# Third and fourth value product by a two-level scheme, and where its rooms and weight sums go

## The chip, the core and the metric

One Trainium2 chip, and one of its cores. The metric is the device time of one execution in microseconds, given as the median of three runs, with one profiled execution beside them.

## The reference

One RWKV block and a gated MLP over 2048 tokens of width 512, all in float32:

```python
x = x + rwkv(layernorm(x))          # time mix, then channel mix
x = x + ffn(layernorm(x))
# time mix: h = LN(x); k, v, r from h mixed with the token before; x += (sigmoid(r) * a/b) @ Wo.T
# channel mix:
h  = LN(x); hh = shift(h)
kk = (h * cm_mk + hh * (1 - cm_mk)) @ Wkey.T        # 512 -> 2048
kv = silu(kk) @ Wval.T                              # 2048 -> 512, the value product
sr = sigmoid((h * cm_mr + hh * (1 - cm_mr)) @ Wcr.T)
x  = x + sr * kv
# ffn: gate, up = h @ w_gate_up.T (512 -> 2 x 2048); out = (silu(gate) * up) @ w_down.T
```

The MLP's weights are other ones than the channel mix's, but the shapes of the value product and of the MLP's down product are the same: 512 tokens by 2048 by 512 in each block.

## The kernel before

The 2048 tokens are four blocks of 512. The kernel first runs time mix and channel mix for all blocks, then the MLP for all blocks. Between the two, each block's result goes to device memory (`resid`) and is loaded again.

**One-level products.** Nearly every product is a `unit` (L539): a Strassen-Winograd scheme of seven products on halves instead of eight. The operands are halves B11, B12, B21, B22 and the differences T1 to T4 (`sums_of`, L464), four VectorE subtractions on 128x512. The weights are halves A11, A12, A22, A21 and the sums S1 to S4. A half product is four matmuls of 128x128 by 256 columns for each of the unit's groups (L558). The value product is a unit with four groups (`down_unit`, L1031), so 7 x 4 x 4 matmuls. Its sink multiplies by the gate and adds to the residual with two `scalar_tensor_tensor` a result.

**Two-level products.** The MLP's down product (`down_product`, L1163) applies the scheme twice. It runs seven half products in the order of `DOWN` (n = 0 to 6), each of them as seven quarter products of four matmuls by 128 columns (L1212). The seven steps of an n are called `first` to `seventh`. They need quarter sums of the operand (`quarter_sums`, L1152: T1, T2, T4 and T3, four subtractions each, written to the tiles `quads` and `quad`, for T3 from n = 2 on in place into `hid`). The sums for n + 2 are asked for in the seventh step of n. A third step reads T2. ScalarE copies each quarter result out of PSUM (L1224), VectorE combines them (`rest`, L1248, and `seventh`), and `summed` (L1166) adds the half results: p1, p3, u2, u4.

Steps six and seven of an n are held back: they are issued between the first and third step of the next n, so that PE runs first(n), sixth(n-1), second(n), seventh(n-1), third(n), fourth(n), fifth(n). The last three products of a `unit` are held back in the same way.

**Weight sums.** The sums S are made on the chip once per weight. `prepare` (L146) loads four pieces on the POOL queue, makes four subtractions on VectorE and stores four pieces to device memory, again on the POOL queue. For a two-level product, each of its weights A11, A12, A22, S1 to S4 gets quarter sums of its own ("dd"), for which the S of the whole weight ("d") come first. Five ticks pass between the loads and the first subtraction. Preparations run in the order of `early` and `late`, at a pace given by `credit` per tick. `need_sums` forces one that is asked for and not ready.

**Who decides the order.** PE, VectorE and ScalarE execute in the order in which the code issues instructions. A planner in the code (`tick`, L295) keeps a slack: each PE step grants 0.88 of its length (1.72 us, half of that in `down_product`) and each VectorE instruction takes its cost off. Background work (norms, mixes) and urgent work (`hot`, the sums) is issued while the slack is above zero. Where a product needs a sum that is not yet issued, `run_one(True)` issues it on the spot, whatever stands before it. Weights arrive on SP's queue into a ring of twelve tiles of 256 KB (`wring`).

**Rooms.** SBUF is given out in pools. `q` (30 tiles of 128x512) and `htp` serve the mixes and are closed after the first gate unit of the MLP (`mixes.close()`, then `last_room`), where the pools of the MLP open: `hidden` (7 large tiles), `quads`, `fq`. Three operand rooms (`opp`) hold mixes, z operands and later the quads; `op_free` lets a mix start only when fewer than three are in use.

## Time and profile before

| | |
|---|---|
| median of three runs | 1238.54 us (1237.72 to 1238.57) |
| profiled execution, first to last instruction | 1237.6 us |
| granted TensorE clock, mean | 0.998 |
| TensorE busy | 1228.9 us, 99% |
| VectorE busy | 711.9 us, 58% |
| ScalarE busy | 358.0 us, 29% |
| moved by DMA | 293.27 MB, 237 GB/s |

The time of the profiled execution is its span, 1237.6 us, from the first to the last instruction; the three runs have their own times, which lie 0.1 to 1.0 us above it. PE is the matmuls, PEld the weight loads that run beside them. A float32 matmul stands as two records in the profile. A group is named by line, engine, operation and tiles, out<-in.

### The profile page before, as it was taken

How to read it: one execution, taken by the hardware profiler on the slowest of the kernel's cores; microseconds unless marked ns; L12 is line 12 of the kernel's file. 1: busy time of each engine (PE TensorE's matmuls, PEld its weight loads, DVE VectorE, ACT ScalarE, POOL GpSimd, SP SyncE). 2: the span in 40 equal slices, each digit the busy share in tenths (PEclk: the TensorE clock that was granted, in tenths of full speed). 3: DMA queues.
4: the chain of work that ended last, by engine and by line, in shares of the span. 5: the costliest groups of instructions: out<-in, count | busy, mean ns of one | idle time of the engine just before them, and what ended most of it. 6: DMA issues, size and time to landing. Idle time of an engine off the chain costs nothing.

```text
span 1237.6 us, 18092 instructions
## 1 busy us (share of the span) xinstructions
PE 1228.9 (99%) x6524; PEld 1101.8 (89%) x6524; DVE 711.9 (58%) x1315; ACT 358.0 (29%) x663; POOL 153.1 (12%) x278
## 2 busy tenths in 40 slices
PE   8999999999999999999999999999999999999998
PEld 7888888888888888888888888998899888998898
DVE  5877686587684757533542365556546365563466
ACT  5534352252532425202311222212221222112211
POOL 1332221222212121222100000000000000000000
PEclk9999999999999999999999999999999999999999
DMA  5768995889877887898756645895459755785576
GB/s 184 255 216 281 311 314 199 307 310 316 276 245 246 291 273 241 261 319 301 248 143 191 215 144 157 270 334 154 143 182 310 271 145 149 239 300 156 153 217 209
DMA packets 139871, 293.27 MB, mean 237 GB/s; under 512 B 17528, under 2 KB 18696, under 8 KB 138504
## 3 DMA queue, kind: packets, MB, share of 16 engines
q1 hardware_dynamic: 116736, 219.20, 56.2%
q0 software_dynamic: 21440, 70.27, 15.5%
q10 hardware_dynamic: 1608, 2.65, 0.6%
q8 instruction: 53, 0.87, 0.3%
q14 instruction: 34, 0.28, 0.1%
HBM read 250.11 MB, written 41.95 MB: 236 GB/s over the span
## 4 chain that ended last, share of the span: by engine, by line
PE 96%; DVE 2%; ACT 1%; DMA 1%; issue 0%; DVEq 0%
PE ps L558 54%; PE ps L1212 14%; PE accv L558 11%; PE accx L558 11%; PE ps L660 5%; PE ps L443 1%; DVE e L395 0%; DMA w<-in_w 0%; DVE mix L395 0%; DMA x<-in_x 0%; ACT mix L873 0%; ACT hT_a L865 0%; DVE q L387 0%; ACT mix L496 0%; DVE st L401 0%; DVE resid L387 0%
## 5 line engine op out<-in xcount | busy, mean ns | idle before, releaser
L558 PE MATMUL ps<-zT,w 128*128 128x256 f32 x1280 | 289.5, 379 | 0.0
L558 PEld LDWEIGHTS ps<-zT,w 128*128 128x128 f32 x1280 | 241.9, 190 | 32.2
L558 PE MATMUL ps<-mix,w 128*128 128x256 f32 x920 | 210.7, 379 | 0.0
L558 PEld LDWEIGHTS ps<-mix,w 128*128 128x128 f32 x920 | 174.5, 190 | 23.6
L387 DVE TENSOR_TENSOR u<-u,accx 128x512 f32<-128x512 f32 x66 | 45.2, 686 | 115.5 <-ACT accx L593 115.5
L1212 PE MATMUL ps<-w,hid 128*128 128x128 f32 x832 | 104.5, 275 | 0.0
L558 PE MATMUL ps<-w,t 128*128 128x256 f32 x456 | 102.2, 379 | 0.0
L1212 PEld LDWEIGHTS ps<-w,hid 128*128 128x128 f32 x832 | 99.8, 192 | 0.8
L558 PEld LDWEIGHTS ps<-w,t 128*128 128x128 f32 x456 | 86.4, 190 | 11.7
L1212 PE MATMUL ps<-w,quads 128*128 128x128 f32 x704 | 89.0, 275 | 0.4 <-ACT r L1224 0.4
L578 ACT COPY accv<-ps 128x512 f32<-128x512 f32 x66 | 37.7, 570 | 176.5 <-PE ps L558 175.4
L1212 PEld LDWEIGHTS ps<-w,quads 128*128 128x128 f32 x704 | 84.2, 192 | 0.9 <-ACT r L1224 0.5
L593 ACT COPY accx<-ps 128x512 f32<-128x512 f32 x66 | 37.7, 571 | 153.7 <-PE ps L558 152.0
L387 DVE TENSOR_TENSOR u<-ps,u 128x512 f32<-128x512 f32 x66 | 45.6, 691 | 62.6 <-PE ps L558 62.2
L387 DVE TENSOR_TENSOR raw<-raw 128x512 f32<-128x512 f32 x92 | 63.3, 688 | 20.1 <-DMA raw<-d 10.7
L589 ACT COPY u<-ps 128x512 f32<-128x512 f32 x66 | 38.6, 585 | 122.9 <-PE ps L558 122.9
L660 PE MATMUL ps<-mix,w 128*128 128x256 f32 x320 | 72.4, 386 | 1.1 <-DVE mix L395 1.1
L1224 ACT COPY r<-ps 128x128 f32<-128x128 f32 x112 | 29.8, 266 | 142.1 <-PE ps L1212 142.1
L660 PEld LDWEIGHTS ps<-mix,w 128*128 128x128 f32 x320 | 61.4, 194 | 10.2 <-DVE mix L395 1.8
L1306 POOL DMA_DIRECT2D out<-resid x12 | 8.6, 716 | 491.5 <-DVE resid L387 491.5
L558 PE MATMUL accv<-zT,w 128*128 128x256 f32 x256 | 60.6, 379 | 0.0
L558 PE MATMUL accx<-zT,w 128*128 128x256 f32 x256 | 60.5, 379 | 0.0
(168 smaller groups left out, 1654.4 us busy)
## 6 DMA issues: line engine op xcount, KB each, us to landing
w<-sum SPq DMA_DIRECT2D x312, 256.0 KB, 3.4
w<-in_w SPq DMA_DIRECT2D x254, 256.0 KB, 3.8
w<-dd SPq DMA_DIRECT2D x112, 256.0 KB, 3.6
raw<-in_w POOLq DMA_DIRECT2D x48, 256.0 KB, 5.5
sum<-raw POOLq DMA_DIRECT2D x48, 256.0 KB, 4.2
w<-d SPq DMA_DIRECT2D x48, 256.0 KB, 3.7
q<-in_w POOLq DMA_DIRECT2D x36, 256.0 KB, 6.3
sum<-q POOLq DMA_DIRECT2D x36, 256.0 KB, 4.7
```

Of the source, the lines that this page charges most:

```text
L387: nc.vector.tensor_tensor(out, a, b, op)
L443: nc.tensor.transpose(flat[:, t * P : (t + 1) * P], h[:, t, c * P : (c + 1) * P], ident)
L558: mm = nc.tensor.matmul(pz[:, m, :], lhsT=lhsT, rhs=rhs, start=first and g == 0 and m == 0 and k == 0, stop=g == last and k == 1, skip_gro ...
L578: "z", A11, B11, True, pop_held, read=lambda: nc.scalar.copy(accv, acc["z"])
L589: nc.scalar.copy(tmp["u2"], acc["z"])
L593: nc.scalar.copy(accx, acc["z"])
L660: mm = nc.tensor.matmul(acc[i, j][:, m, :], lhsT=act[:, k, lo] if by_token else wg[:, k, lo], rhs=wg[:, k, :] if by_token else act[:, k, : ...
L1212: mm = nc.tensor.matmul(dst, lhsT=x[k][:, g, :], rhs=wt[:, g, :], start=first and g == 0, stop=g == 3, skip_group_check=True,)
L1224: nc.scalar.copy(st["r"][:, m, n * P : (n + 1) * P], st["z"])
L1306: eng.dma_start(out_t[b][:, tokens, cols], rs[b][:, tokens, cols])
```

## The change

The value product of blocks 2 and 3 (`b >= DEEP`) goes through `down_product`, with quarter weights of its own: `wv` (quarters of the four halves, laid out on the host), `vsum` (the S sums of the four value weights, stored so that quarters can be read from them as pieces of 128 columns) and "vv" (the quarter sums). The seven "vv" preparations stand ahead of the MLP's in `late`. The MLP's preparations are no longer all forced before the MLP starts but go on in it. `credit` is 1.0 from block 2's gate unit to the end of its up units and the same in block 3, 0 during the two products, and 1.0 in the MLP. In block 2, after the gate unit and the next block's out unit, the mix pools close and the rooms for `hidden` and `quads` open, with waits by tile; one operand room goes to the quads from there on. Gates, and from block 3 on e and t tiles, come from the pool `up`, which grows from 6 to 10 tiles; `q` shrinks from 30 to 25. The first MLP operand (`ffn_in(0)`) is pushed after the first up unit of block 3 instead of after the last.

```diff
-    up = ctx.enter_context(tc.tile_pool(name="up", bufs=6))
+    up = ctx.enter_context(tc.tile_pool(name="up", bufs=10))
+    prep = ctx.enter_context(tc.tile_pool(name="prep", bufs=6))
...
+    vsum = [
+        dram.tile([P, 4, 2, HB], F32, tag=f"vsum{s}", name=f"vsum{s}") for s in range(4)
+    ]
+    for g in range(4):
+        sums[WVAL + g] = [flat(t[:, g]) for t in vsum]
+
+    def value_part(q, k):
+        if q < 4:
+            return wv[q, k].rearrange("p (g c) -> p g c", c=P)
+        m, kk = divmod((0, 1, 3, 2)[k], 2)
+        return vsum[q - 4][:, :, kk, m * P : (m + 1) * P]
+
+    for q in (A11, A12, A22, S1, S2, S3, S4):
+        sources["vv", q] = [value_part(q, k) for k in range(4)]
+        sums["vv", q] = scratch(f"vv{q}", 4)
...
+    def value_weight(q, k):
+        if k >= 4:
+            need_sums(("vv", q))
+            return ring(sums["vv", q][k - 4]).rearrange("p a (h c) -> p (a h) c", c=P)
...
+        nc.sync.dma_start(t, value_part(q, k))
+        return t
...
+    def value_up(b, g):
+        hid = hidden.setdefault((b, "v"), {})
+        def sink(i, j, c):
+            q = (B11, B12, B21, B22)[2 * i + j]
+            if q not in hid:
+                hid[q] = hidden_tile()
+            nc.scalar.activation(hid[q][:, g], c, AF.Silu)
+            if g == 3:
+                made.add(((b, "v"), q))
+                if q in (B11, B22):
+                    quarter_sums((b, "v"), 0 if q == B11 else 1)
...
     def up_unit(b, g):
+        if b >= DEEP:
+            value_up(b, g)
+            return
...
+        if b >= DEEP:
+            down_product((b, "v"), sink, value_weight, False, done)
+            return
         unit([WVAL + g for g in range(4)], [Lazy((b, g)) for g in range(4)], sink, True, done)
...
+    def deep_room():
+        def pool(stack, name, bufs):
+            return stack.enter_context(
+                tc.tile_pool(name=name, bufs=bufs, reuse_waits="tile")
+            )
+        room["hidden"] = pool(ctx, "hidden", 7)
+        more = pool(ctx, "more", 1)
+        ctx.enter_context(middle)
+        pools["ht"] = pool(middle, "htl", 1)
+        m, _ = op_tile("quads")
...
-    late = [n + g for g in range(4) for n in (WG, WU)] + [("dd", A11)]
+    late = [("vv", q) for q in (A11, S4, S2, A12, S1, S3, A22)]
+    late += [n + g for g in range(4) for n in (WG, WU)] + [("dd", A11)]
...
+        if b >= DEEP:
+            credit[1] = 1.0
         gate_unit(b)
         if b + 1 < NB:
             out_unit(b + 1)
+        if b == DEEP:
+            need((b, "ck"))
+            mixes.close()
+            deep_room()
...
+            if b == NB - 1 and g == 0:
+                push((0, "z", "t"), ffn_in(0), op_free)
...
-        if b == NB - 1:
-            push((0, "z", "t"), ffn_in(0), op_free)
+        if b >= DEEP:
+            credit[1] = 0.0
         down_unit(b)
...
-    while preps:
-        need_sums(preps[-1][0])
+    credit[1] = 1.0
     need((0, "z"))
     ffn_gate(0, 0)
-    mixes.close()
     last_room()
```

In the changed kernel the matmul lines L558 and L1212 are L600 and L1312, the VectorE add and subtract L387 is L429, `scalar_tensor_tensor` L395 is L437, and the copy out of PSUM L1224 is L1324.

More of the change, by code (lines that the diff above doesn't have):

```diff
@@ L35 @@
 TURNED = 2
+DEEP = 2
 PLAIN = {(0, WK), (0, WR), (0, WV), (0, WO), (1, WK), (1, WR)}
@@ L69, in rwkv_ffn_kernel @@
     wd: bass.AP,
+    wv: bass.AP,
     out: bass.AP,
@@ L90, in rwkv_ffn_kernel, with ht_tile @@
     mixes = ctx.enter_context(ExitStack())
-    htp = mixes.enter_context(tc.tile_pool(name="htp", bufs=2))
-    prep = mixes.enter_context(tc.tile_pool(name="prep", bufs=6))
-    pools = {"q": mixes.enter_context(tc.tile_pool(name="qp", bufs=30))}
+    pools = {
+        "ht": mixes.enter_context(tc.tile_pool(name="htp", bufs=2)),
+        "q": mixes.enter_context(tc.tile_pool(name="qp", bufs=25)),
+    }
+    def ht_tile(name):
+        return pools["ht"].tile([P, NC, TB + 1], F32, tag="hT", name=name)
     def q_tile(name):
@@ L150, in prepare @@
             t = prep.tile([P, 2, HB], F32, tag="raw", name="raw") if own else q_tile("q")
-            paced(nc.gpsimd.dma_start(flat(t), sources[n][k]))
+            src = sources[n][k]
+            dst = flat(t)
+            if len(src.shape) == 3:
+                dst = dst.rearrange("p (g c) -> p g c", c=P)
+            paced(nc.gpsimd.dma_start(dst, src))
             raw.append(t)
@@ L186, in down_weight @@
         return ring(src).rearrange("p a (h c) -> p (a h) c", c=P)
+    def value_weight(q, k):
+        if k >= 4:
+            need_sums(("vv", q))
+            return ring(sums["vv", q][k - 4]).rearrange("p a (h c) -> p (a h) c", c=P)
+        if q >= 4:
+            for g in range(4):
+                need_sums(WVAL + g)
+        t = wring.tile([P, 2, HB], F32, tag="w", name="w")
+        t = t.rearrange("p a (h c) -> p (a h) c", c=P)
+        nc.sync.dma_start(t, value_part(q, k))
+        return t
     def load_x(b, queues=None):
@@ L768, in time_norm @@
         yield from scaled(xb, h, mv, both)
-        hT = htp.tile([P, NC, TB + 1], F32, tag="hT", name="hT_a")
+        hT = ht_tile("hT_a")
         hTs[b, "a"] = hT
@@ L804, in turned_norm @@
         tails[b] = residual(b, xb, [(mv[:, t, 0:1], rstd[:, t : t + 1]) for t in range(NT)])
-        hT = htp.tile([P, NC, TB + 1], F32, tag="hT", name="hT_a")
+        hT = ht_tile("hT_a")
         hTs[b, "a"] = hT
@@ L825, in first_block @@
         xb = xin.pop(0)
-        hT = htp.tile([P, NC, TB + 1], F32, tag="hT", name="hT_a")
+        hT = ht_tile("hT_a")
         hTs[0, "a"] = hT
@@ L928, in sink @@
                 ts(r[:, o, :], c[:, o, :], nfirst[:, n : n + 1], 0.0, ALU.subtract, ALU.min)
-            e = q_tile("e")
+            e = (u_tile if b > DEEP else q_tile)("e")
             q[i, j] = e
@@ L953, in hidden_sums @@
             for t in (T1, T2, T4):
-                B[t] = q_tile("t")
+                B[t] = (u_tile if key[0] > DEEP else q_tile)("t")
             B["sums"] = set()
@@ L983, in rwkv_ffn_kernel @@
     gates = {}
+    wide = []
     def channel_norm(b):
@@ L994, in channel_norm @@
         yield from scaled(x1, h, mv, rstd)
-        hT = htp.tile([P, NC, TB + 1], F32, tag="hT", name="hT_b")
+        hT = ht_tile("hT_b")
         hTs[b, "b"] = hT
@@ L1004, in sink @@
         def sink(i, j, c):
-            s = q_tile("sr")
+            if b == DEEP:
+                if not wide:
+                    wide.append(tok_tile("sr"))
+                s = wide[0][:, 2 * i + j, :].rearrange("p (m c) -> p m c", m=2)
+            else:
+                s = u_tile("sr")
             nc.scalar.activation(s, c, AF.Tanh, scale=0.5)
@@ L1009, in gate_unit @@
         product_of(b, WCR, "cr", sink, True)
+    def value_up(b, g):
[9 more added lines that the diff above has]
+                    quarter_sums((b, "v"), 0 if q == B11 else 1)
+        unit(
+            [WKEY + g],
+            [Lazy((b, "ck"))],
+            sink,
+            False,
+            lambda: hidden_done((b, "v"), g),
+            op_done if g == 3 else None,
+        )
     def up_unit(b, g):
+        if b >= DEEP:
+            value_up(b, g)
+            return
         s = {}
@@ L1085, in ffn_gate @@
         s = gated[b, g] = {}
-        tile_of = u_tile if (b, g) == (0, 0) else q_tile
+        tile_of = q_tile if g % 2 else u_tile
         def sink(i, j, c):
@@ L1108, in sink, with hidden_done @@
                     quarter_sums(b, 0 if q == B11 else 1)
-        def done():
-            if g == 0:
-                for t in (T1, T2, T4):
-                    hid[t] = hidden_tile()
-            urgent((b, "f", g), sums_of({t: hid[t][:, g] for t in hid}))
-            if g == 3:
-                made.update((b, t) for t in (T1, T2, T4, "T3"))
-        unit([WU + g], [Lazy((b, "z"))], sink, False, done, op_done if g == 3 else None)
+        unit(
+            [WU + g],
+            [Lazy((b, "z"))],
+            sink,
+            False,
+            lambda: hidden_done(b, g),
+            op_done if g == 3 else None,
+        )
+    def hidden_done(b, g):
+        hid = hidden[b]
+        if g == 0:
+            for t in (T1, T2, T4):
+                hid[t] = hidden_tile()
+        urgent((b, "f", g), sums_of({t: hid[t][:, g] for t in hid}))
+        if g == 3:
+            made.update((b, t) for t in (T1, T2, T4, "T3"))
     hidden, made, asked = {}, set(), set()
@@ L1128, in hidden_tile @@
         return room["hidden"].tile([P, 4, 2, HB], F32, tag="hid", name="hid")
-    def last_room():
-        room["hidden"] = ctx.enter_context(tc.tile_pool(name="hidden", bufs=7))
-        pools["q"] = ctx.enter_context(tc.tile_pool(name="fq", bufs=15))
-        more = ctx.enter_context(tc.tile_pool(name="more", bufs=1))
+    middle = ExitStack()
+    def deep_room():
+        def pool(stack, name, bufs):
+            return stack.enter_context(
+                tc.tile_pool(name=name, bufs=bufs, reuse_waits="tile")
+            )
+        room["hidden"] = pool(ctx, "hidden", 7)
+        more = pool(ctx, "more", 1)
+        ctx.enter_context(middle)
+        pools["ht"] = pool(middle, "htl", 1)
         m, _ = op_tile("quads")
@@ L1139, in last_room @@
         room["sets"] = tiles[:4], tiles[4:]
+    def last_room():
+        middle.close()
+        pools["q"] = ctx.enter_context(
+            tc.tile_pool(name="fq", bufs=4, reuse_waits="tile")
+        )
     def quarters(t):
@@ L1161, in quarter_sums, with down_product @@
         urgent((b, "quarters", n), run())
-    def down_product(b, sink, final):
+    def down_product(b, sink, weight_of, final, done=None):
         base = {}
@@ L1195, in summed @@
                 sink(1, 0, base["u2"])
+                if done is not None:
+                    done()
         def steps(n):
@@ L1209, in product @@
                         run_one(True)
-                wt = down_weight(a, q)
+                wt = weight_of(a, q)
                 for g in range(4):
@@ L1318, in sink @@
                 store(0, slice(HB, HB + P))
-        down_product(b, sink, final)
+        down_product(b, sink, down_weight, final)
     early = [WV, WCR, WO] + [WKEY + g for g in range(4)] + [WVAL, WVAL + 1]
-    late = [n + g for g in range(4) for n in (WG, WU)] + [("dd", A11)]
+    late = [("vv", q) for q in (A11, S4, S2, A12, S1, S3, A22)]
+    late += [n + g for g in range(4) for n in (WG, WU)] + [("dd", A11)]
     late += [("d", k) for k in range(4)] + [("dd", q) for q in (S4, S2, A12, S1, S3, A22)]
@@ L1363, in rwkv_ffn_kernel @@
             out_unit(b + 1)
+        if b == DEEP:
+            need((b, "ck"))
+            mixes.close()
+            deep_room()
         need((b, "ck"))
@@ L1457, in _layout @@
     )
+    down = val
+    wv = np.stack(
+        [np.stack([quarter_quarter(i, j, m, k) for m, k in places]) for i, j in places]
+    )
     return {
@@ L1463, in _layout @@
         "wd": np.ascontiguousarray(wd),
+        "wv": np.ascontiguousarray(wv),
     }
```

## The prediction

> **What bounds it now.** I read the busy times first, then the chain that ended last, then stretches, then the order in time of one two-level product. Page, part 1:

> ```profile
> PE 1228.9 (99%) x6524; PEld 1101.8 (89%) x6524; DVE 711.9 (58%) x1315; ACT 358.0 (29%) x663; POOL 153.1 (12%) x278
> ```

> PE is busy all through; DVE has room on average. So time falls only where PE gets less to do, and rises where PE is made to wait. The chain of work that ended last, in order of time, gives PE's pace for the two matmul widths:

> ```profile
> 594.60 6.91 PE ps L558 x32
> ...
> 778.62 39.30 PE ps L1212 x352
> ...
> 920.92 39.30 PE ps L1212 x352
> ```

> L558 is the 256-column matmul of a one-level unit: 6.91 / 32 = 215.9 ns a record (two records to a matmul). L1212 is the 128-column one of the two-level product: 39.30 / 352 = 111.6 ns, back to back for 39 us. Half the width costs 0.517 of the time.

> The stretches of the third value product (first line) and of the first MLP down product (second), columns as PE, PEld, DVE, ACT, POOL, clock, DMA share, GB/s:

> ```profile
> 503.00:552.00 49.00, 49.00 (x229) 43.14 (x228) 19.56 (x30) 5.30 (x9) 10.23 (x19) 1.00 0.88 300
> 778.62:817.92 39.30, 39.30 (x354) 39.30 (x353) 25.55 (x48) 7.02 (x25) 1.98 (x3) 1.00 0.90 297
> ```

> Neither stretch has a PE gap. The two-level form keeps DVE 65% busy and DMA at 0.90; both were affordable there.

> **What PE saves.** A value product is 7 products x 4 groups x 4 matmuls = 112 of 256 columns, 224 records: 224 x 215.9 ns = 48.4 us. At two levels it is 49 x 4 = 196 of 128 columns, 392 records: 392 x 111.6 = 43.8 us. That is 4.6 us saved in each, 9.2 us in blocks 2 and 3. The order of the built kernel confirms the counts (224 fewer 256-column matmuls, 392 more 128-column ones) and changes no other PE work.

> **What DVE gets.** Per product: 28 quarter sums of 0.69, seven each of 0.29, 0.29 and 0.425 for combining, seven adds of 0.69: 31 us, less the unit's two u2 operations (1.4 us). Once: seven preparations of four subtractions, 28 x 0.69 = 19.3 us, with 56 more POOL DMA issues of 0.54 us. In all 2 x 29.8 + 19.3 = 79 us, to about 64% of the span. The preparations go ahead of the MLP's, in block 1 and the start of block 2, where DVE was about 70% busy; the MLP's move back by as much, and the last eight end during the MLP of block 0 (32 subtractions, 22 us, in 99 us that hold 51 us of DVE work: 76.65 in the stretch 778 to 921 less 25.55). No weight is asked for before its preparation ended in the built order, so neither PE nor SP waits for one: 0. If that cover failed, a wait like the longest now on a preparation's load (9.8 us, DVE for raw<-d) would stand before the gated products; PE rode through it then, and with DVE fuller perhaps 5 us would reach PE.

> **Where the order makes PE wait.** Now the same stage of an MLP down product, n = 6 (it starts at 811.51), in order of time; DVE:

> ```profile
> 809.03 0.29 DVE L387 TENSOR_TENSOR r<-ps,r 128x128 f32<-128x128 f32 x1 [1.05 <-PE ps L1212]
> 809.42 1.42 DVE L387 TENSOR_TENSOR r<-r 128x512 f32<-128x512 f32 x2
> 810.88 0.69 DVE L387 TENSOR_TENSOR resid<-r,resid 128x512 f32<-128x512 f32 x1
> 811.49 0.69 DVE L387 TENSOR_TENSOR quads<-hid 128x512 f32<-128x512 f32 x1
> 812.21 1.42 DVE L387 TENSOR_TENSOR quads<-hid,quads 128x512 f32<-128x512 f32 x2
> ...
> 815.28 0.29 DVE L387 TENSOR_TENSOR r<-ps,r 128x128 f32<-128x128 f32 x1 [0.33 <-PE ps L1212]
> 815.68 0.69 DVE L387 TENSOR_TENSOR r<-r 128x512 f32<-128x512 f32 x1
> 816.41 0.69 DVE L387 TENSOR_TENSOR resid<-r,resid 128x512 f32<-128x512 f32 x1
> 817.01 0.69 DVE L387 TENSOR_TENSOR r<-r 128x512 f32<-128x512 f32 x1
> ```

> and PE:

> ```profile
> 811.51 2.84 PE L1212 MATMUL ps<-w,hid 128*128 128x128 f32 x24
> 814.19 1.95 PE L1212 MATMUL ps<-w,quads 128*128 128x128 f32 x16
> ```

> The quarter sums for n = 6 (quads, 811.49 to 813.6) end 1.5 us before the third quarter product, which reads T2 and starts at 815.08, right behind the seventh of n = 5. The adds that belong to that seventh (815.28 on) come after them. In block 2's value product DVE has more: each result costs two scalar_tensor_tensor (0.69 each) where the MLP has one add, and the second channel mix of block 3 falls into it, since the quads tile holds one of three operand rooms. The planner runs out of slack and the built order differs: for n = 6, T1 stands early but T2 stands *behind* the seventh of n = 5 and all its adds. From the seventh's end, with the spacings of the rows above: 0.20 to the first add, 0.40 to u4, 0.73 to sr (reads u4), 0.73 to x (reads sr), 0.60 to u2, 0.60 to T2, 0.69 for T2, 0.1 to load it as PE's weights: 4.05 us, in which PE has nothing else queued that may run. For n = 5 only T3 stands late: 0.20 + 0.40 + 3 x 0.73 + 0.60 + 0.68 + 0.1 = 4.17 us against four quarter products of 0.893 = 3.57: 0.6 us. Block 3's product has no mix beside it; there T2 for n = 6 is ordered ahead of the seventh of n = 5 and by the same spacings ends 1.5 us early: 0. So 4.65 us are given back. Bounds: 0 if DVE overlaps more than the rows show, 7 if DVE enters the stage 2 us late.

> **The half clock.** Granted clock, windows of the start:

> ```profile
> 7.60:11.00 3.40, 1.55 (x9) 1.12 (x10) 2.73 (x10) 1.85 (x4) 0.97 (x2) 1.00 1.05 389
> 11.00:14.40 3.40, 3.40 (x9) 2.71 (x9) 2.28 (x5) 2.11 (x5) 0.07 (x1) 0.51 0.78 288
> ```

> A stretch in which PE was busy 1.55 of 3.40 us was followed by 3.4 us at half clock, which costs 1.7 us of work. A 4.05 us gap may do the same: 0 to 1.7 us. I take 0 and give the 1.7 to a rival: of that row's nine PE records eight are transposes (L860), so it says how little matmul work brings the half clock, and a gap that falls across two such windows leaves up to 1.4 us of matmuls in each.

> [...]

> **DMA.** SP loads 42 more weights, 49 instead of 28 per product, the rate that the MLP's products hold. New is that 12 of the 49 read the S sums as 512-byte pieces, 512 packets instead of 128. The page's queue part gives q1 116736 packets in 56.2% of 16 engines' span, 95 ns each (mostly 2 KB). In the last 4.6 us (DMA view) there are 512- and 1024-byte stores:

> ```profile
> q1 hardware_dynamic: 432, 0.26, 17.8%
> ```

> 17.8% x 16 x 4.6 us / 432 = 30 ns. So a load in 512-byte pieces takes 512 x 30 / 16 = 0.96 us against 128 x 95 / 16 = 0.76: 12 x 0.2 = 2.4 us in 43.8, share 0.90 to 0.95; the ring of twelve weights gives some 9.8 us of lead. I take 0.

> [...]

> **Rooms.** The hidden, quads and q tiles take over memory of tiles whose last readers ran before; the gates, e and t tiles move to the larger u pool. Cover: up_unit's 12.1 us of PE per unit; without it a late Silu of 0.6 us per tile, under 2 us.

> **Sum.** The profiled execution: span 1237.6; the three runs (median 1238.54) lie 0.1 to 1.0 above. 1237.6 - 9.2 + 4.65 = 1233.05; with the median's 0.9 on top, 1234.0.

> **Rivals.** (a) The order's waits mostly vanish (DVE ahead of PE): 1229.3 to 1232. For: DVE is idle 1.05 us before the seventh's add in the MLP. Against: in-order DVE, T2 behind five dependent ops. (b) The half clock in full, or DVE 2 us late at the gap: 1235.5 to 1236.5. For: the row at 0.51; against: its transposes. (c) DVE held by a preparation's load in block 0's MLP, 5 us: 1239, no change. For: the 9.8 us wait; against: PE had no gap in it. (d) Slower: loads of 512-byte pieces fall behind. If such a packet cost as much as a 2 KB one (95 ns) a load takes 3.0 us, 12 x 2.3 = 27 us more in each product; spare time 4.4 and lead 9.8 leave 13 us of PE waiting twice: 1260. It decides from about 60 ns a packet ((4.4 + 9.8) / 12 = 1.2 us more a load, 1.95 in all), twice the row's, which speaks against it; for it speaks that these are reads, which the row is not. (e) The product is not faster at two levels: against it, 39.30 us per 352 records.

> **Chances.** Forecast (1232 to 1235.5) 0.47, (a) 0.14, (b) 0.20, (c) 0.10, (d) 0.08, (e) 0.01. A measurement of this kernel tells 0.2% (2.5 us) from no change. Faster by more than that (under 1236.1): 0.47 + 0.14 + 0.18 = 0.79; same: 0.02 of (b) + 0.09 of (c) = 0.11; slower: 0.10. Leaving out about 0.1 at each end, the range reaches from (a)'s lower part, 1230, to 1238.

> **What would show it.** In the profile after: two stretches of about 43.8 us with L1312 in blocks 2 and 3; one PE gap near 4 us late in the first, released by DVE quads, none in the second; clock 1.00 or 0.5 for 3.4 us just behind it. Wrong if no such gap is there, if PE waits for w<-vsum loads, or if gaps appear in the MLP of block 0.

## The result, and the profile after

| | before | after |
|---|---|---|
| median | 1238.65 us (1237.39 to 1239.42) | 1240.95 us (1238.46 to 1242.76) |
| ratio to before | | 1.0018 [1.001, 1.0026] |
| profiled span | 1237.6 us | 1239.1 us |
| granted clock, mean | 0.998 | 0.997 |

Medians are over 14 runs each, side by side. The changed kernel is 2.3 us slower; 4.5 us faster was forecast, and the time lies outside the range, on the other side.

The page of the changed kernel: busy time by engine, then groups with their busy time, mean duration and the idle time before them with its releaser, then DMA issues with their median time to landing.

```profile
PE 1222.6 (99%) x6860; PEld 1106.7 (89%) x6860; DVE 784.1 (63%) x1451; ACT 368.7 (30%) x713; POOL 186.7 (15%) x334
...
L600 PE MATMUL ps<-zT,w 128*128 128x256 f32 x1280 | 289.5, 379 | 2.4 <-ACT accx L635 2.4
...
L1312 PE MATMUL ps<-w,quads 128*128 128x128 f32 x1056 | 135.5, 278 | 4.2 <-DVE quads L429 3.8
...
L429 DVE TENSOR_TENSOR raw<-raw 128x512 f32<-128x512 f32 x120 | 82.5, 687 | 47.8 <-DMA raw<-d 12.9
...
w<-vsum SPq DMA_DIRECT2D x56, 256.0 KB, 4.3
w<-vv SPq DMA_DIRECT2D x56, 256.0 KB, 4.2
```

PE's busy time fell by only 6.3 us (at half clock a matmul counts as busy for longer: 8 records take 2.08 us at 549.55 below, at full clock 1.06 at 544.65), and two waits are new: 3.8 us for the quarter sums (DVE quads) in a two-level product, and 2.4 us for a ScalarE copy (L635) in the first products of the MLP. The chain that ended last, in order of time, shows both:

```profile
508.42 33.96 PE ps L1312 x304
542.79 2.93 PE ps L1312 x24
549.55 5.45 PE ps L1312 x24
...
621.73 39.30 PE ps L1312 x352
...
714.22 6.31 DMA raw<-in_wd
723.33 1.99 PE ps L600 x8
```

Block 3's product runs its 352 records back to back in 39.30 us, as the MLP's products did before. Block 2's stops at 542.79 and 549.55, and its last 24 records take 5.45 us, where 24 at full pace take 2.68. Order of time around the second stop, first DVE, then PE:

```profile
545.75 0.29 DVE L429 TENSOR_TENSOR r<-ps,r 128x128 f32<-128x128 f32 x1 [1.73 <-PE ps L1312]
546.14 0.69 DVE L429 TENSOR_TENSOR r<-r 128x512 f32<-128x512 f32 x1
546.87 0.69 DVE L437 SCALAR_TENSOR_TENSOR sr<-sr,r 128x512 f32<-128x512 f32 x1
547.60 0.69 DVE L437 SCALAR_TENSOR_TENSOR x<-sr,x 128x512 f32<-128x512 f32 x1
548.21 0.69 DVE L429 TENSOR_TENSOR r<-r 128x512 f32<-128x512 f32 x1
548.81 1.41 DVE L429 TENSOR_TENSOR quads<-hid,quads 128x512 f32<-128x512 f32 x2
...
549.55 2.08 PE L1312 MATMUL ps<-w,quads 128*128 128x128 f32 x8 [3.84 <-DVE quads L429]
551.41 1.92 PE L1312 MATMUL ps<-w,hid 128*128 128x128 f32 x8
```

This is the forecast wait: five instructions that stand before T2 in DVE's order, then T2, then PE. What lies behind it was put at nothing. The clock's records in this trace last 542.72 us at 1.00, 6.83 us at 0.50 (from 548.00 on) and 682.67 us at 1.00, which is 159, 2 and 200 times 3.413 us. Windows on that grid (columns as in the prediction):

```profile
544.60:548.00 3.40, 1.11 (x10) 0.92 (x9) 2.08 (x4) 0.00 (x0) 0.00 (x0) 1.00 0.84 262
548.00:551.40 3.40, 1.85 (x8) 1.85 (x9) 2.78 (x5) 0.00 (x0) 0.00 (x0) 0.50 0.04 14
551.40:554.80 3.40, 3.40 (x18) 3.40 (x17) 0.00 (x0) 0.27 (x1) 0.00 (x0) 0.50 0.33 87
554.80:558.20 3.40, 3.40 (x22) 3.12 (x21) 2.69 (x6) 1.10 (x3) 0.96 (x2) 1.00 0.75 257
```

The clock is 0.50 for two windows. PE has work for half clock from 549.55 to 554.8, which is 2.6 us lost.

The other new wait, in the MLP of block 0, all engines in order of time:

```profile
713.69 1.07 POOL L180 DMA_DIRECT2D raw<-in_wd  x2 [3.12 <-issue]
...
715.58 5.34 PE L600 MATMUL ps<-zT,w 128*128 128x256 f32 x24
720.61 1.42 DVE L429 TENSOR_TENSOR raw<-raw 128x512 f32<-128x512 f32 x2 [6.33 <-DMA raw<-in_wd]
...
721.94 0.68 DVE L429 TENSOR_TENSOR hid<-accx,s 128x512 f32<-128x512 f32 x1
...
722.71 0.57 ACT L635 COPY accx<-ps 128x512 f32<-128x512 f32 x1 [8.08 <-DVE hid L429]
...
723.33 1.99 PE L600 MATMUL ps<-zT,w 128*128 128x256 f32 x8 [2.42 <-ACT accx L635]
```

Read it backwards: PE waits for ScalarE to free a PSUM tile, ScalarE for DVE's gated product, and DVE, in order, stands at a preparation's subtraction until a load lands. The page blames ACT; the wait begins with the load, which POOL issued only at 713.69. The chain puts the store of the preparation before (dd<-raw, 4.25 us) ahead of it, and then 2.86 us for which it names nothing. That the load's tile was still held by that preparation is argued from the code (six tiles, four a preparation); no row shows it. A smaller stop at 688 us (1.05 us) is PE's own wait for a weight (w<-sum), in the stretch where DMA moves 389 GB/s.

**Accounts.** A stop is counted here from where the last records would have ended at full pace, so that it comes out up to 0.3 us longer than the idle time that a view gives in brackets. From the trace, PE's stops beyond its matmul pace: 0.60 and 4.00 us in block 2's product, 1.05 (688 us) and 2.68 (720 us) in block 0's MLP, 0.60 at 318 us in block 1. With 2.6 us of half clock the losses are 11.5 us. Over the runs, a time lies mostly some 1.8 us above its span, so the span of a median run before is 1236.8: 1236.8 - 9.2 + 11.5 = 1239.1, the span after. Experiments had to show whether these terms are real.

### The profile page after: what moved, and what is told of

The parts are those of the page before. It is cut to its first block, busy times and chain, and to the rows that moved or that the text cites. A ratio compares the mean times of both kernels' runs of the same rounds, so it can differ in the third digit from the quotient of the medians.

```text
span 1239.1 us, 19206 instructions
## 1 busy us (share of the span) xinstructions
PE 1222.6 (99%) x6860; PEld 1106.7 (89%) x6860; DVE 784.1 (63%) x1451; ACT 368.7 (30%) x713; POOL 186.7 (15%) x334
## 3 DMA queue, kind: packets, MB, share of 16 engines
q1 hardware_dynamic: 132000, 230.22, 58.6%
## 4 chain that ended last, share of the span: by engine, by line
PE 88%; DMA 5%; DVE 3%; issue 2%; ACT 1%; POOL 0%; ACTq 0%; DVEq 0%; POOLq 0%
PE ps L600 43%; PE ps L1312 21%; PE accx L600 9%; PE accv L600 9%; PE ps L702 4%; PE ps L485 1%; DMA raw<-d 1%; DMA raw<-in_wd 1%; DMA dd<-raw 1%; DMA d<-raw 1%; DMA raw<-in_w 1%; DMA row<-stats 1%; DVE e L437 0%; DVE h L433 0%; DVE st L443 0%
## 5 line engine op out<-in xcount | busy, mean ns | idle before, releaser
L600 PE MATMUL ps<-zT,w 128*128 128x256 f32 x1280 | 289.5, 379 | 2.4 <-ACT accx L635 2.4
L600 PEld LDWEIGHTS ps<-zT,w 128*128 128x128 f32 x1280 | 241.8, 190 | 34.8 <-ACT accx L635 2.8
L600 PE MATMUL ps<-mix,w 128*128 128x256 f32 x920 | 211.0, 379 | 0.0
L600 PEld LDWEIGHTS ps<-mix,w 128*128 128x128 f32 x920 | 174.1, 190 | 23.3
L1312 PE MATMUL ps<-w,hid 128*128 128x128 f32 x1248 | 157.9, 276 | 0.4 <-ACT r L1324 0.4
L1312 PEld LDWEIGHTS ps<-w,hid 128*128 128x128 f32 x1248 | 150.7, 193 | 1.8 <-ACT r L1324 0.6
L1312 PE MATMUL ps<-w,quads 128*128 128x128 f32 x1056 | 135.5, 278 | 4.2 <-DVE quads L429 3.8
L1312 PEld LDWEIGHTS ps<-w,quads 128*128 128x128 f32 x1056 | 128.1, 194 | 5.1 <-DVE quads L429 4.0
L429 DVE TENSOR_TENSOR raw<-raw 128x512 f32<-128x512 f32 x120 | 82.5, 687 | 47.8 <-DMA raw<-d 12.9
L1324 ACT COPY r<-ps 128x128 f32<-128x128 f32 x168 | 44.5, 265 | 211.4 <-PE ps L1312 211.4
L429 DVE TENSOR_TENSOR u<-u,accx 128x512 f32<-128x512 f32 x64 | 43.8, 684 | 74.4 <-ACT accx L635 74.4
L429 DVE TENSOR_TENSOR hid<-hid 128x512 f32<-128x512 f32 x126 | 84.7, 686 | 2.4 <-DVE hid L429 0.5
L635 ACT COPY accx<-ps 128x512 f32<-128x512 f32 x64 | 36.5, 570 | 130.8 <-PE ps L600 115.5
L429 DVE TENSOR_TENSOR r<-ps,r 128x256 f32<-128x256 f32 x83 | 29.7, 359 | 69.7 <-PE ps L1312 65.3
L429 DVE TENSOR_TENSOR u<-ps,u 128x512 f32<-128x512 f32 x64 | 44.1, 689 | 46.3 <-PE ps L600 42.7
L600 PE MATMUL accx<-zT,w 128*128 128x256 f32 x256 | 60.6, 380 | 0.8 <-DMA w<-sum 0.8
L600 PE MATMUL accv<-zT,w 128*128 128x256 f32 x256 | 60.6, 380 | 0.0
L429 DVE TENSOR_TENSOR quads<-hid,quads 128x512 f32<-128x512 f32 x84 | 58.1, 692 | 2.8
```

What stands on the lines that cost most here:

```text
L429: nc.vector.tensor_tensor(out, a, b, op)
L600: mm = nc.tensor.matmul(pz[:, m, :], lhsT=lhsT, rhs=rhs, start=first and g == 0 and m == 0 and k == 0, stop=g == last and k == 1, skip_gro ...
L635: nc.scalar.copy(accx, acc["z"])
L1312: mm = nc.tensor.matmul(dst, lhsT=x[k][:, g, :], rhs=wt[:, g, :], start=first and g == 0, stop=g == 3, skip_group_check=True,)
L1324: nc.scalar.copy(st["r"][:, m, n * P : (n + 1) * P], st["z"])
```

## Experiments

Theory 1: the saving is there in full, and three losses cover it: the order's waits in block 2's product, the half clock that they set off, and DVE held by preparations in block 0's MLP. Rivals: two levels save less than counted, the gaps only move, or the short DMA pieces cost.

**Quarter sums first** (`e1_sums_first`): the sums of n + 2 are issued ahead of n's adds in block 2's product.

```diff
                 if n + 2 < 7:
                     quarter_sums(b, n + 2)
+                    while b == (DEEP, "v") and (b, "quarters", n + 2) not in finished:
+                        run_one(True)
                 summed(n, r)
```

> Block 2's value product issues the four quarter sums of n + 2 ahead of the adds of n; nothing else moves, PE's order is the same. Theory 1 (order): T2 for n = 6 then ends before the seventh step of n = 5, so the 4.0 us and 0.6 us gaps go, and with them the half clock behind them (6.83 us in the profile, about 2.6 us of work): 1240.95 - 7.2 = 1233.7 us, clock 1.00 through the product. Rival 2 (the quarter sums are late for lack of DVE time, not for their place): the waits come back at other steps and the time stays within 2 us of 1241.

Measured: 1234.49 us, ratio 0.997 [0.9961, 0.9979]. Order of time, DVE and PE of the same place:

```profile
541.00 0.68 DVE L429 TENSOR_TENSOR quads<-hid 128x512 f32<-128x512 f32 x1
...
541.72 1.42 DVE L429 TENSOR_TENSOR quads<-hid,quads 128x512 f32<-128x512 f32 x2
...
545.25 1.95 PE L1312 MATMUL ps<-w,quads 128*128 128x128 f32 x16
...
547.04 1.06 PE L1312 MATMUL ps<-w,hid 128*128 128x128 f32 x8
```

T2 now ends over 2 us ahead of its reader and PE has no stop here; moving DVE instructions alone gains some 6 us. A stop of 2.45 us near 715 us remained in the MLP, and it too brought the half clock (second window):

```profile
715.20:718.60 3.40, 1.21 (x6) 0.99 (x6) 3.33 (x6) 1.06 (x2) 1.82 (x4) 1.00 0.69 256
718.60:722.00 3.40, 3.40 (x10) 2.69 (x9) 3.30 (x8) 0.60 (x1) 2.48 (x5) 0.50 0.86 289
```

**The gap filled** (`e2_gap_filled`): fourteen matmuls on the identity in the gap, otherwise the changed kernel.

```diff
+                if b == (DEEP, "v") and n == 6:
+                    for _ in range(14):
+                        nc.tensor.matmul(flat(accv)[:, :P], lhsT=ident, rhs=ident,
+                            start=False, stop=True, skip_group_check=True)
```

> The changed kernel with 14 matmuls of 128 columns on the identity (28 records, 3.1 us) put on PE ahead of the third step of n = 6 in block 2's value product, into a bank that is not in use. They take nothing away. Theory 1 (the gap itself lowers the clock): the wait for T2 stays as long, but PE works in it, the clock stays 1.00 and 2.6 us come back: 1238.3 us. Rival (the clock falls for another reason than idleness, or the loss is not the clock's): half clock stays, 1241 us or a little more.

Measured: 1239.67 us, ratio 1.0008 [0.9998, 1.0017]. The clock stayed at 1.00 in the product, but in the profile the 2.36 us stop in the MLP now brought a half clock that it had not brought in the profile of the changed kernel. The time agrees with neither value well: 1.3 us gained. This was repeated below without that stop.

**No late sums** (`e3_no_late_sums`): the last ten preparations of the MLP's down weights are left out, and plain quarters of the weight are loaded in place of the sums, so the MLP's result is another one.

```diff
-        if k >= 4:
-            need_sums(("dd", q))
-            src = sums["dd", q][k - 4]
-        elif q >= 4:
-            need_sums(("d", k))
-            src = sums["d", k][q - 4]
-        else:
-            src = wd[q, k]
+        src = wd[q % 4, k % 4]
...
-    late += [("d", k) for k in range(4)] + [("dd", q) for q in (S4, S2, A12, S1, S3, A22)]
```

> Leaves out the last ten weight preparations (those of the MLP's down product but the first) and loads plain weight quarters in their place, so the MLP's result is not the reference's; loads on SP keep number and size. Theory 1: the 1.05 and 2.7 us PE gaps in the MLP of block 0 come from VectorE waiting in order for the preparations' loads, so they go: 1240.95 - 3.7 = 1237.2 us. Rival (SP's own loads or the fuller VectorE make them): a gap of 1 us or more stays there, 1239.5 us or above.

Measured: 1237.51 us, ratio 0.999 [0.998, 0.9999]. The MLP's stops are gone, the 4.00 us stop in block 2's product stays, 3.4 us gained. Its windows show where the clock falls:

```profile
545.60:549.00 3.40, 1.56 (x14) 1.36 (x13) 1.67 (x3) 0.07 (x1) 0.00 (x0) 1.00 0.86 287
549.00:552.40 3.40, 1.40 (x12) 1.41 (x13) 3.20 (x6) 0.21 (x1) 0.00 (x0) 1.00 0.16 57
552.40:555.90 3.50, 3.50 (x17) 3.32 (x17) 0.29 (x1) 0.32 (x2) 0.00 (x0) 0.51 0.52 150
```

The gap straddles two windows, PE is at work for over 40% of each (1.56 and 1.40 of 3.40 us), and yet the clock falls to 0.51 behind the second.

**Both** (`e4_both`): the edits of `e1_sums_first` and `e3_no_late_sums`.

> e1's order and e3's omission together. Theory 1: all three losses go and only the shorter PE work is left: 1240.95 - 10.9 = 1230.0 us, that is 8.6 us under the kernel before (9.2 counted less a few tenths). Rival (the two-level product does not save 9.2 us, DMA or weight loads slow it): 1233 us or above with no PE gap over 0.5 us.

Measured: 1230.34 us, ratio 0.9935 [0.9922, 0.9947]; no stop in the MLP, and no half clock while PE is at work. This is 8.3 us under before (by the interval 6.6 to 9.7), of 9.2 counted, and two stops of 0.5 and 0.8 us are left that before has not (319 and 218 us): two levels save what they were said to.

**Slower pace** (`e5_slower_pace`): sums first as above, all the arithmetic kept, and the MLP's preparations paced at 0.6.

```diff
-    credit[1] = 1.0
+    credit[1] = 0.6
     need((0, "z"))
```

> The quarter sums come first in block 2's product, and the preparations of the last MLP are paced at 0.6 a tick in place of 1.0 once the MLP begins, so that one finds fewer of its tiles still being stored. Theory 1 (DVE is held by a preparation's load behind stores, and PE with it): the gap of 2.4 us near 715 us and the half clock behind it shrink or go, 1231 to 1232.5 us. Rival (any preparation at this place runs into the late load, whatever the pace): the gap only moves, 1234.5 us, as the version with the sums first and nothing else.

Measured: 1231.61 us, ratio 0.9944 [0.9932, 0.9957]: with nothing left out it is 7 us faster than before, 9 faster than the changed kernel. Two windows of block 0's MLP, in the changed kernel:

```profile
680.00:690.00 10.00, 9.22 (x43) 7.82 (x42) 1.38 (x2) 2.87 (x5) 1.07 (x2) 1.00 1.03 389
...
710.00:725.00 15.00, 12.58 (x59) 10.77 (x58) 8.49 (x17) 2.56 (x5) 4.03 (x9) 1.00 0.87 294
```

and in this version:

```profile
680.00:690.00 10.00, 10.00 (x48) 8.79 (x48) 2.01 (x4) 2.57 (x5) 1.77 (x4) 1.00 1.04 391
...
710.00:725.00 15.00, 15.00 (x71) 13.19 (x71) 11.77 (x31) 3.51 (x6) 3.28 (x7) 1.00 0.88 289
```

PE is busy all through, at the same rate of DMA (391 and 389 GB/s), so the rate alone did not stop PE. That it is the place and time of a preparation's load is argued from the waits above, and tested by the next versions. This profile is of the slowest of the five runs and has stops of up to 1.4 us elsewhere (164, 220, 321 and 600 us).

**Preparations in block 3's product** (`e6_prep_in_product`): sums first in both products, and preparations go on in block 3's.

```diff
-                    while b == (DEEP, "v") and (b, "quarters", n + 2) not in finished:
+                    while isinstance(b, tuple) and (b, "quarters", n + 2) not in finished:
...
-            credit[1] = 0.0
+            credit[1] = 0.4 if b > DEEP else 0.0
```

> The quarter sums come first in both value products, and the preparations go on at 0.4 a tick during block 3's product, whose DVE has room and whose DMA is light; five remain for the MLP of block 0 in place of eight. Theory 1 (the loss in that MLP is the crowd of preparations, loads of the residual and weights): the MLP keeps at most one short gap, 1230.5 to 1232.5 us. Rival (DVE in the product is as full as in block 2's, and the preparations make it late there): gaps in block 3's product, 1234 us or more.

Measured: 1245.96 us, ratio 1.0054 [1.0041, 1.0067]: theory 1 failed here, and the rival has only a part of it. PE is idle for 1.65 us in block 3's product (648 us, released by DVE quads), and stops in the MLP for 4.28 (684 us) and 2.80 us (701 us), with 10.2 us at half clock behind them. Order of time near the largest:

```profile
674.15 1.06 POOL L180 DMA_DIRECT2D raw<-in_wd  x2 [2.41 <-issue]
...
677.21 7.07 PE L600 MATMUL ps<-zT,w 128*128 128x256 f32 x32
...
685.57 1.42 DVE L429 TENSOR_TENSOR raw<-raw 128x512 f32<-128x512 f32 x2 [12.91 <-issue]
...
688.29 3.78 PE L600 MATMUL accv<-zT,w 128*128 128x256 f32 x8 [4.02 <-ACT accv L620]
```

The chain gives the load from 674.15 a landing after 10.33 us, in the stretch where DMA is at its fullest. Fewer preparations in the MLP did not help. The rows suggest that it matters where one of them falls, and whether DVE reaches its subtraction before the load has landed; the next version tests the second.

**The same with a longer lead** (`e7_prep_and_lead`): in the MLP eight ticks in place of five between loads and subtraction.

```diff
-                item[1] = WAIT
+                item[1] = lead[0]
...
+    lead[0] = 8
     need((0, "z"))
```

> As the version with preparations in block 3's product, and in the MLP eight ticks in place of five lie between a preparation's loads and its subtraction, some 16 us in place of 10. Theory 1: DVE finds every load landed, no gap in block 0's MLP, 1229.8 to 1231 us. Rival (the MLP's gaps come from the weights' own loads at over 350 GB/s, not from DVE's wait): the same as the version without the longer lead, within 0.5 us.

Measured: 1235.58 us, ratio 0.9971 [0.9961, 0.9981]. The MLP's stops are gone, as theory 1 has it, and 10 us with them; the total missed, since the lead is longer in the MLP alone and block 3's product stops for 3.2 us, with 3.4 us of half clock behind it:

```profile
647.69 1.42 DVE L430 TENSOR_TENSOR raw<-raw 128x512 f32<-128x512 f32 x2 [8.47 <-DMA raw<-d]
...
650.69 1.67 PE L1313 MATMUL ps<-w,quads 128*128 128x128 f32 x8 [3.04 <-DVE quads L430]
```

**Long pieces** (`e8_long_pieces`): as `e6_prep_in_product`, with the weights that were read in 512-byte pieces replaced by plain ones in 2 KB pieces.

```diff
-        nc.sync.dma_start(t, value_part(q, k))
+        nc.sync.dma_start(t, value_part(q % 4, k))
```

> As the version with preparations in block 3's product, and the third-quadrant weights of the two value products are loaded from the plain value weight in pieces of 2,048 bytes in place of the summed weight in pieces of 512 bytes; the product is of other weights, so the result is not the reference's. Theory 1 (the short pieces cost nothing, as taken): the same time as that version within 0.5 us. Rival (short pieces hold up the queue of the weights): faster by 1 us or more.

Measured: 1246.21 us, ratio 1.0055 [1.0042, 1.0067], within 0.3 us of `e6_prep_in_product`, with 122784 packets on q1 in place of 132000, though the stops of the two fall somewhat differently. The five runs of each spread over some 2.5 us, so a cost below 1 or 2 us would not show; none shows.

**Pace alone** (`e9_pace_alone`): the changed kernel with the credit of 0.6 in the MLP and nothing else.

> The changed kernel with the preparations of the last MLP at 0.6 a tick and nothing else; the quarter sums stay behind the adds. Theory 1 (the losses add up: waits of 4.6 us in block 2's product and one or two windows of half clock behind them, 1.7 or 2.6 us, and nothing more): 1231.6, the version with sums first and the same pace, + 6.3 to 7.2, so 1237.5 to 1239 us, with the 4.0 us gap near 545 us, a half clock behind it and no gap near 715 us. Rival (what the pace gained came from the sums' place too): gaps in block 0's MLP as before the pace was cut, 1241 us.

Measured: 1237.42 us, ratio 0.9989 [0.998, 0.9998]. No stop above 0.3 us in the MLP (the one at 688 us is gone too), the 4.00 us stop in block 2's product as before, and a half clock of 3.4 us behind it. The MLP's term is 3.5 us, as `e3_no_late_sums` had it.

**Pace, and the gap filled** (`e10_pace_and_filled`): the edits of `e9_pace_alone` and `e2_gap_filled`.

> As the version with the slower pace alone, and 14 small matmuls, 28 records, fill the 4.0 us gap of block 2's product, so that PE waits just as long for the sums but is at work meanwhile; they change no result. Theory 1 (the half clock is a loss of its own, set off by the idle stretch): the clock stays at 1.00 and the time falls by one to two windows at half pace, 1.7 to 2.6 us below the version with the slower pace alone, 1235.5 to 1237 us. Rival (the half clock costs nothing that the wait has not cost already): the same time within 0.5 us.

Measured: 1235.61 us, ratio 0.9973 [0.9962, 0.9984]. Order of time on PE, then the windows of the gap, those of `e9_pace_alone` first:

```profile
545.82 3.29 PE L1339 MATMUL accv<-ident 128*128 128x128 f32 x28
549.82 1.16 PE L1312 MATMUL ps<-w,quads 128*128 128x128 f32 x8 [0.70 <-DVE quads L429]
```

```profile
546.60:550.10 3.50, 0.66 (x5) 0.66 (x6) 3.40 (x7) 0.00 (x0) 0.00 (x0) 0.99 0.36 134
550.10:553.50 3.40, 3.40 (x18) 3.40 (x17) 0.62 (x2) 0.27 (x1) 0.00 (x0) 0.50 0.29 77
```

```profile
547.00:550.40 3.40, 2.69 (x24) 2.50 (x24) 3.30 (x6) 0.00 (x0) 0.00 (x0) 1.00 0.42 154
550.40:553.80 3.40, 3.40 (x28) 3.27 (x27) 1.29 (x4) 0.53 (x2) 0.00 (x0) 1.00 0.43 125
```

PE's useful work starts again at 549.82 as it did (549.44 in the profile of `e9_pace_alone`; in both 6.75 us after the start that ends the small stop before), but at full clock: 1.8 us gained, about one window at half pace (3.41 / 2 = 1.7), though this profile has a stop of 1.41 us at 686 us, on a weight's load, that the other has not. The medians are of 11 and 7 runs that spread over 3.8 and 1.8 us, so the size is known only roughly; the granted clocks of the single runs agree on the cause, 0.996 to 0.998 in the eleven and 0.998 to 1.000 in the seven. The half clock was a loss of its own here, 1.8 us beside the wait that set it off.

## Why the prediction was wrong, point by point

- **What PE saves, 9.2 us: right.** `e4_both` has 8.3 of it beside 1.3 us of other stops; block 3's product takes 39.30 us per 352 records, the pace of the sum.
- **The order's waits, 4.05 + 0.6 us: right.** The trace has 4.00 and 0.60. The page names DVE's quarter sums for the first, as forecast. For the second it names a ScalarE copy, which ended 0.02 us before the forecast T3 (hid, 542.69); `e1_sums_first` moves DVE alone and has no stop there, which speaks for T3. Together with their half clock they are worth 6.5 us (1240.95 to 1234.49) or 5.8 (1237.42 to 1231.61).
- **Block 3's product, 0: right**, 39.30 us without a stop.
- **The half clock, taken as 0: wrong.** The step failed where the row (1.55 us of work in 3.40, then 0.51) was set aside as a matter of transposes, which no run shows to count for less, and where a gap across two windows was taken to be safe. The row held: the half clock measured 2.6 us in the profile and 1.8 over the runs of `e10_pace_and_filled` against `e9_pace_alone`.
- **The cover of the preparations, taken as 0: wrong.** The fallback of the same step, perhaps 5 us, named the right chain (DVE at a preparation's load before the gated products); it measured 3.5 us. Gaps in that MLP were among the prediction's own signs of being wrong. The step looked at DVE's average in the MLP, 22 us of subtractions in 99, where most of the loss comes from a single wait of 6.3 us on a load that was issued late; 1.05 us of it is a weight's load in the crowded stretch before. That the kernel before had no stop in this MLP proved nothing about the cover: its preparations had ended before the MLP began.
- **DMA, 512-byte pieces, 0: right.** w<-vsum lands in 4.3 us, w<-vv in 4.2; `e8_long_pieces` shows no gain, to within 1 or 2 us.
- **Rooms, 0:** no wait of PE on them stands in the trace; the runs did not take them apart. Of the 0.60 us stop at 318 us in block 1 the cause was not tried: the chain leads from it over ScalarE and DVE to a load of 6.66 us (row<-stats), and it stands, 0.5 to 1.4 us long, in every changed version and not in the kernel before.
- **From span to median, 0.9 us: off by as much.** A run's time lies 1.8 us above its span, and the profile of before was slower than its median run by some 0.8 us, with a half clock of 3.4 us at the start that the profile after lacks (clock 0.96 and 1.00 from 0 to 40 us). The two cancel in the sum, by luck. So 2.6 us of half clock, 3.5 us in the MLP and 0.6 us in block 1 make 6.7 of the 6.95 us by which 1240.95 lies above the forecast of 1234.0.
- **Rivals.** (b) and (c) were priced as if one excluded the other. Both came true, on top of the forecast: 1234.0 + 1.7 + 5 = 1240.7 by their own prices, and 1240.95 was measured. That this agrees so well is luck: the half clock was priced too low by the profile (1.7 against 2.6) and the MLP too high (5 against 3.5). They should have been terms with chances, added together; the range would then have reached 1241. (d), the only slower case given, was not what made it slower.

## What to carry to other kernels

Where one engine serves both the main work and a background task in the order of the code, as DVE does here, cost the background task by its worst wait at the place where it will run, not by its share of busy time: one subtraction that stood 6.33 us at a late load held the gated product behind it, and 2.42 us of that reached PE. When PE is the bound, a stop of some 2.4 us or more should be charged with about 1.7 us of half clock on top (ten of twelve such stops had it here, and 1.8 us came back where one was filled). The losses from different places added up here, to 6.7 of 6.95 us, so let a forecast add them too; and what a change loses may be had back by order and pace alone, 9.3 us here, with no arithmetic changed.
